# Second group norm of block 0: statistics as row sums instead of a statistics instruction

## The chip, the cores and the metric

The kernel runs on one core of a Trainium2 chip. A core has five engines that run side by side, each with its own in-order queue: TensorE (PE, matrix products), VectorE (DVE), ScalarE (ACT), GpSimd (POOL) and SyncE (SP), which here issues the DMAs. They wait for each other through semaphores. The metric is the time of one execution on the device, in microseconds; before the change the median of three runs is 7226.67 us.

## The reference

The input x is 4 images of 128 channels and 128 x 128 pixels, float32. Two layers follow each other.

Layer 0 turns an image into a sequence of 16384 tokens of 128 channels, sends it through a small MLP, an input projection, a causal convolution of 4 taps and a selective scan, and then

```
g  = out.reshape(B, 4, 32, H, W)
xn = (g - g.mean) * rsqrt(g.var + 1e-5)          # first group norm, 4 groups
x1 = silu(xn * gn_w + gn_b) + x
```

Layer 1 needs, beside a filter in the Fourier domain, one set of 4 weights for each image:

```
a = group_norm(concat([x1, x1]))                 # second group norm: 32 groups over 256 channels
a = relu(agg_w @ a + agg_b);  pooled = a.mean    # then a softmax over 4 logits
```

So the second group norm wants, for each channel of x1, its mean and its variance over 16384 pixels; channels are then combined to groups.

## The kernel before

The kernel has two blocks. Block 0 (line 150 on) computes layer 0 and, while a later image is scanned, also the first group norm, x1, the second group norm and the softmax weights of the image before. Block 1 computes the Fourier part; the last image's norms run there.

Block 0 works in chunks of 512 tokens, 32 for an image and 128 in all, numbered k. A chunk is cut into 16 slots. In each slot two tiles of 128 x 512 are scanned. The order of all instructions is written out by hand: lists `todo[slot, phase]` are filled first, and a double loop (L503 to L506) then issues slot after slot and, in a slot, phase after phase in the order of L504: turn, sums, pe, exps, late, act, pool, dbu, early, gate, scans, dve, end. Each engine sees its own instructions in that order. Slot numbers below count within a chunk.

What a slot does on each engine:
- ScalarE: the exponentials for the next slot's scans (`exps`, L392), small copies of scan states (L414 and L506), and whatever the phase act holds: activations of the next chunk, two for each (L238 u in slot 2, L252 xd in slot 4, L455 and L456 o in slot 5, L274 delta in slot 6, L303 bt in slots 8 to 14).
- VectorE: two scans (L411), and in odd slots mostly two products of a scanned tile with C (L413); the copies of L414 on ScalarE wait for them. In slots 2 and 10 a gating product (L442).
- GpSimd: products for the scans to come (`dbu`, L362) and products of scanned tiles with C that VectorE doesn't do (L418), and in slot 7 `du` (L311).
- TensorE: the projections, transposes and the sums over the state.

Which tiles' products VectorE takes is decided by `by_vector` (L346). In the chunks where the norm runs (`norming`, L337: k from 34 to 49, 66 to 81, 98 to 113) VectorE takes one product fewer than otherwise.

The norm of an image is `finish` (L560). It is called for images 0 to 2 in block 0 (L488 to L490) and for image 3 in block 1. It first calls `group_norm` (L509) for the first norm; its row sums and sums of squares come from `o_act` (L455 and L456), where ScalarE accumulates while it copies. Then, for each of 32 tiles i of 128 x 512, two tiles to a chunk: `norm_load` brings x and the layer's output from DRAM (slots 13 and 14 of the chunk before); `norm_act` (slot 2) applies scale, bias and Silu on ScalarE, into a PSUM bank; `norm_dve` (slot 3, phase dve) adds x on VectorE and stores x1 to DRAM; `norm_stats` (slot 3, phase end) runs one statistics instruction on the sum on VectorE (L593). Six numbers per tile are kept in `stats1`. Five slots after the last addition `group_norm` is called for the second norm: `aggregate` (L519) turns the 32 x 6 numbers into mean and variance on VectorE (L522), `mean_mm` multiplies by a matrix that averages over groups, and so on to the scale. For the first norm, `aggregate` adds up the 32 pairs of sums (L524), and `mean_mm` first forms mean and variance from them with four small operations on ScalarE (L529 to L532).

Of the kernel before, what the change touches and what calls it, by code (L numbers as in the profile page):

```python
# [26 lines left out]
F32 = mybir.dt.float32  # L27
AF = mybir.ActivationFunctionType
ALU = mybir.AluOpType
AX = mybir.AxisListType  # L30
# [3 lines left out]
P = 128  # L34
# [471 lines left out]
                        f()  # L506


def group_norm(s, io, b, mat, which, stat, at, then):  # L509


    nc = s.nc
    g = {}

    def small(n, m=1):
        g[n] = io.small.tile([P, m], F32, tag=n, name=f"{n}_{which}_{b}")
        return g[n]

    def aggregate():  # L519
        mv = small("mv", 2)  # L520
        if which:
            nc.vector.bn_aggr(mv, stat().rearrange("p n q -> p (n q)"))  # L522
        else:
            nc.vector.reduce_sum(mv, stat(), axis=AX.X)  # L524

    def mean_mm():
        if which == 0:
            mv, q = g["mv"], small("q")
            nc.scalar.activation(q, mv[:, 0:1], AF.Square, scale=1.0 / s.L)  # L529
            nc.scalar.mul(q, q, -1.0)  # L530
            nc.scalar.mul(mv[:, 0:1], mv[:, 0:1], 1.0 / s.L)
            nc.scalar.activation(mv[:, 1:2], mv[:, 1:2], AF.Identity, scale=1.0 / s.L, bias=q)  # L532
        ps = g["ps"] = io.psum(f"gm_{which}_{b}")
        nc.tensor.matmul(ps[:, 0:1], getattr(s, mat), g["mv"][:, 0:1], start=True, stop=True)

    def spread_act():
        mv = g["mv"]
        nc.scalar.copy(small("mean"), g["ps"][:, 0:1])
        q = small("q")
        nc.scalar.activation(q, mv[:, 0:1], AF.Square, scale=-1.0, bias=g["mean"])  # L540
        nc.scalar.activation(q, q, AF.Identity, bias=mv[:, 1:2])

    def var_mm():
        ps = g["ps"] = io.psum(f"gv_{which}_{b}")
        nc.tensor.matmul(ps[:, 0:1], getattr(s, mat), g["q"], start=True, stop=True)

    def root_act():
        nc.scalar.activation(small("rstd"), g["ps"][:, 0:1], AF.Sqrt, bias=s.eps)

    def invert():  # L550
        nc.vector.reciprocal(g["rstd"], g["rstd"])
        then(g["mean"], g["rstd"])

    return [
        (at, "dve", aggregate), (at, "end", mean_mm), (at + 1, "act", spread_act), (at + 3, "pe", var_mm),
        (at + 5, "act", root_act), (at + 6, "dve", invert),
    ]


def finish(s, io, b, first, norm, agg, add="dve"):  # L560

    nc, NCH, C, L, NF = s.nc, s.NCH, s.C, s.L, s.NF
    stats, outs = s.stats, s.outs
    g = {}

    def start(mean, rstd):
        for n in ("scale", "bias"):
            g[n] = io.small.tile([P, 1], F32, tag=n, name=f"{n}_{b}")  # L570
        nc.scalar.activation(g["scale"], s.gnw, AF.Identity, scale=rstd)
        nc.scalar.activation(g["bias"], mean, AF.Identity, scale=g["scale"])
        nc.scalar.activation(g["bias"], g["bias"], AF.Identity, scale=-1.0, bias=s.gnb)
        g["stat"] = io.small.tile([P, NCH, 6], F32, tag="stats1", name=f"stats1_{b}")

    def norm_load(i):
        xr = g["x", i] = io.big.tile([P, T], F32, tag="xr", name=f"xr_{b}_{i}")
        o = g["o", i] = io.big.tile([P, T], F32, tag="o", name=f"of_{b}_{i}", bufs=io.bufs)
        nc.sync.dma_start(out=xr, in_=s.xflat[b, :, i * T : (i + 1) * T])
        nc.sync.dma_start(out=o, in_=outs[b][:, i * T : (i + 1) * T])  # L580

    def norm_act(i):

        g["n", i] = io.psum(f"n_{b}_{i}")
        nc.scalar.activation(g["n", i], g["o", i], AF.Silu, bias=g["bias"], scale=g["scale"])

    def norm_dve(i):
        o = g["o", i]
        nc.vector.tensor_add(o, g.pop(("n", i)), g.pop(("x", i)))
        nc.sync.dma_start(out=s.x1flat[b][:, i * T : (i + 1) * T], in_=o)  # L590

    def norm_stats(i):
        nc.vector.bn_stats(g["stat"][:, i, :], g.pop(("o", i)))  # L593

    def middle(mean, rstd):
        g["mean"] = mean
        g["weff"] = io.small.tile([P, C], F32, tag="weff", name=f"weff_{b}")
        nc.scalar.activation(g["weff"], s.weff0, AF.Identity, scale=rstd)
        g["acc"] = io.small.tile([P, NCH], F32, tag="acc", name=f"acc_{b}")

    def bias_mm():
        g["ps"] = io.psum(f"bv_{b}")
        nc.tensor.matmul(g["ps"][:, 0:1], g["weff"], g["mean"], start=True, stop=True)

    def bias_act():
        g["bv"] = io.small.tile([P, 1], F32, tag="bv", name=f"bv_{b}")
        nc.scalar.activation(g["bv"], g["ps"][:, 0:1], AF.Identity, scale=-1.0, bias=s.bias0)

    def agg_load(i):
        x1 = g["x1", i] = io.big.tile([P, T], F32, tag="xr", name=f"x1_{b}_{i}")  # L610
        nc.sync.dma_start(out=x1, in_=s.x1flat[b][:, i * T : (i + 1) * T])

    def agg_mm(i, home):
        ps = g["pa", i] = (home or io.psum)(f"agg_{b}_{i}")
        nc.tensor.matmul(ps, g["weff"], g.pop(("x1", i)), start=True, stop=True)  # L615

    def agg_act(i):
        ps = g.pop(("pa", i))
        nc.scalar.activation(ps, ps, AF.Relu, bias=g["bv"], accum_out=g["acc"][:, i : i + 1])

    def pool_dve():
        g["pooled"] = io.small.tile([P, 1], F32, tag="pooled", name=f"pooled_{b}")
        nc.vector.reduce_sum(g["pooled"], g["acc"], axis=AX.X)

    def pool_act():
        g["pbc"] = io.small.tile([P, P], F32, tag="pbc", name=f"pbc_{b}")
        nc.scalar.activation(g["pbc"], s.ones, AF.Identity, scale=g["pooled"])

    def logits_mm():
        g["ps"] = io.psum(f"lg_{b}")  # L630
        nc.tensor.matmul(g["ps"][:, 0:NF], g["pbc"], s.wwg, start=True, stop=True)

    def logits_dve():
        lg = g["lg"] = io.small.tile([P, NF], F32, tag="lg", name=f"lg_{b}")
        mx = g["mx"] = io.small.tile([P, 1], F32, tag="mx", name=f"mx_{b}")
        nc.vector.scalar_tensor_tensor(lg, g["ps"][:, 0:NF], 1.0 / L, s.bwg, ALU.mult, ALU.add)
        nc.vector.reduce_max(mx, lg, axis=AX.X)

    def softmax_act():
        mx, lg = g["mx"], g["lg"]  # L640
        nc.scalar.mul(mx, mx, -1.0)
        total = g["total"] = io.small.tile([P, 1], F32, tag="total", name=f"total_{b}")
        nc.scalar.activation(lg, lg, AF.Exp, bias=mx, accum_out=total)

    def softmax_dve():
        nc.vector.reciprocal(g["total"], g["total"])

    def weights_act():
        nc.scalar.activation(s.wts[b], g["lg"], AF.Identity, scale=g["total"])

    todo = group_norm(s, io, b, "g0", 0, lambda: stats[b], first, start)
    for i in range(NCH):
        at = norm(i)
        todo += [
            (at[0], "pe", partial(norm_load, i)), (at[1], "act", partial(norm_act, i)),
            (at[2], add, partial(norm_dve, i)), (at[2], "end", partial(norm_stats, i)),
        ]
    c = at[2] + 5
    todo += group_norm(s, io, b, "g1", 1, lambda: g["stat"], c, middle)
    todo += [(c + 7, "pe", bias_mm), (c + 8, "act", bias_act)]  # L660
    for i in range(NCH):
        at = agg(i)
        todo += [
            (at[0], "dve", partial(agg_load, i)), (at[1], "pe", partial(agg_mm, i, at[3])),
            (at[2], "act", partial(agg_act, i)),
        ]
    c = at[2] + 1
    return todo + [
        (c, "dve", pool_dve), (c + 1, "act", pool_act), (c + 4, "pe", logits_mm), (c + 4, "dve", logits_dve),
        (c + 5, "act", softmax_act), (c + 6, "dve", softmax_dve), (c + 7, "act", weights_act),  # L670
    ]


def block1(tc, s):
# [7 lines left out]
    nc, B, C, H, W, WF, NF, NCH = s.nc, s.B, s.C, s.H, s.W, s.WF, s.NF, s.NCH  # L682
    HH = H // 2
    filt = s.a["filt_w"].rearrange("f c h w q -> h f c (w q)")
    with ExitStack() as ctx:
        def pool(name, bufs, **kw):
# [15 lines left out]
        io = SimpleNamespace(  # L702
            big=pool("big", 4), bufs=4, small=small, psum=lambda n: psf.tile([P, T], F32, tag="pf", name=f"pf_{n}")
        )
# [4 lines left out]

        t1 = norm(NCH - 1)[2] + 14  # L710
        todo = defaultdict(list)
        steps = finish(s, io, B - 1, 0, norm, lambda i: (t1 + i - 3, t1 + i, t1 + i, None), "add")
        for at, phase, f in steps:
            todo[at, phase].append(f)
        spare = max(at for at, _ in todo) // 3 + 2
# [23 lines left out]
        for k, ft in enumerate(spans):  # L739
            at = max(ft.first - 4, min(k, 1))  # L740
# [243 lines left out]
```

## Time and profile before

| | |
|---|---|
| median of three runs | 7226.67 us (7223.53 to 7229.71) |
| the profiled execution: span from its first to its last instruction | 7219.4 us |
| VectorE busy | 6925.4 us (96%), 8040 instructions |
| GpSimd busy | 6890.8 us (95%), 3188 instructions |
| ScalarE busy | 6133.6 us (85%), 13583 instructions |
| TensorE busy | 5935.8 us (82%) |
| the addition L589: in block 0, in block 1 | 96 at 678 ns, 32 at 681 ns |
| the statistics L593: both blocks | 128 at 681 ns |
| a scan, L411 (the largest group) | 1976 at 1265 ns |

The profiled execution has no time of its own beside its span; what a run has around the span is to be seen only as the difference to the median, 7.3 us. Busy time leaves out the waiting of an engine, so an engine at 96% over the whole may have no idle time at all in one stage; durations of neighbours overlap by a little, so what an instruction costs is better read from one start to the next than from its length.

### The profile page before, as it was taken

Reading aid. Unit: us, or ns where it says so; the run is one execution under the profiler, and the core shown is the slowest. Engines: PE = TensorE matmul, PEld = TensorE weight load, DVE = VectorE, ACT = ScalarE, POOL = GpSimd, SP = SyncE. Lnnn points to the kernel's source line nnn. Section 1 sums busy time; section 2 is a strip of 40 time slices with the busy share of each in tenths; the row PEclk is TensorE's granted clock in tenths of the full one; section 3 lists DMA queues with packets and bytes.
Section 4 is the critical chain, followed back from the end, with each engine's and each line's share of the span. In section 5 each row is a group of like instructions: output and inputs, shape, how many; then the busy total and the mean of one; then the engine's idle time right before and its main releaser. Section 6 shows DMA issues by size and latency. Waiting matters only on the chain. (4 is left out here: it accounts for less than half of the span.)

```text
span 7219.4 us, 89408 instructions
## 1 busy us (share of the span) xinstructions
PE 5935.8 (82%) x25908; PEld 2629.2 (36%) x25908; DVE 6925.4 (96%) x8040; ACT 6133.6 (85%) x13583; POOL 6890.8 (95%) x3188
## 2 busy tenths in 40 slices
PE   7888888888878788888788788887787888868999
PEld 2333333322222233332222233332232323348999
DVE  7999999999999999999999999999999999978677
ACT  7888888888888888888888888888888888877876
POOL 7999999999999999999999999999999999977787
PEclk8888888888888898998888899998888898989999
DMA  6766676677777776777777777777787777768666
GB/s 151 160 159 160 151 165 159 151 165 172 180 192 178 182 172 161 175 169 170 190 179 192 174 160 176 171 160 187 179 192 181 169 173 169 161 167 240 183 169 164
DMA packets 864127, 1246.27 MB, mean 173 GB/s; under 512 B 78856, under 2 KB 318608, under 8 KB 863632
## 3 DMA queue, kind: packets, MB, share of 16 engines
q1 hardware_dynamic: 863488, 1240.28, 71.8%
q8 instruction: 204, 3.34, 0.2%
q14 instruction: 291, 2.38, 0.1%
q10 hardware_dynamic: 144, 0.26, 0.0%
HBM read 996.97 MB, written 243.27 MB: 172 GB/s over the span
## 5 line engine op out<-in xcount | busy, mean ns | idle before, releaser
L362 POOL TENSOR_TENSOR hb<-rdu,rB 128x1536 f32<-128x1536 f32 (+2 forms) x1536 | 3608.0, 2366 | 35.1 <-DMA rdu<-dd 32.1
L392 ACT ACTIVATE da<-rdelta,amat 128x512 f32<-128x512 f32 x4096 | 2786.1, 698 | 139.3 <-DVE h L411 134.5
L418 POOL TENSOR_TENSOR hb<-h,rC 128x1024 f32<-128x1024 f32 (+1 forms) x1072 | 2436.8, 2275 | 68.4 <-DVE h L411 53.9
L411 DVE TENSOR_TENSOR_SCAN da<-da,st,hb 128x512 f32<-128x512 f32 x1976 | 2417.4, 1265 | 22.1 <-ACT da L392 15.6
L432 PE MATMUL y<-hb,sel 128*32 128x512 f32 x8192 | 1337.9, 730 | 4.7 <-POOL hb L418 4.1
L382 PE MATMUL b<-ident,bt 128*128 128x128 f32 x4096 | 753.9, 307 | 673.5 <-DVE h L411 539.1
L413 DVE TENSOR_TENSOR hb<-da,rC 128x512 f32<-128x512 f32 x2040 | 1294.3, 672 | 3.0
L411 DVE TENSOR_TENSOR_SCAN h<-da,st,b 128x512 f32<-128x512 f32 x992 | 1256.2, 1266 | 1.5 <-PE b L382 1.5
L411 DVE TENSOR_TENSOR_SCAN h<-da,st,hb 128x512 f32<-128x512 f32 x1000 | 1249.9, 1254 | 1.4 <-ACT da L392 1.0
L233 PE MATMUL pp_cv<-xm,wck 128*128 128x512 f32 x2048 | 1061.0, 665 | 1.4 <-ACT xm L216 0.8
L303 ACT ACTIVATE bt<-pt_dut,xdt 128x256 f32<-128x256 f32 x2048 | 836.3, 470 | 186.0 <-PE pt_dut L292 185.8
L382 PEld LDWEIGHTS b<-ident,bt 128*128 128x128 f32 x4096 | 525.5, 154 | 1242.1 <-DVE h L411 902.5
L414 ACT COPY st<-da 128x1 f32<-128x1 f32 x2040 | 271.3, 159 | 495.0 <-DVE hb L413 494.7
L233 PEld LDWEIGHTS pp_cv<-xm,wck 128*128 128x128 f32 x2048 | 417.3, 215 | 706.5 <-issue 460.8
L767 POOL TENSOR_TENSOR wb<-wb,term 128x1040 f32<-128x1040 f32 x192 | 461.1, 2402 | 89.8 <-ACT term L761 78.6
L292 PE MATMUL pt_dut<-ident,du 128*128 128x128 f32 x1024 | 233.7, 339 | 299.9 <-ACT xdt L285 174.0
L428 PE MATMUL y<-u,diag 128*128 128x512 f32 x512 | 300.9, 671 | 149.7 <-DVE zs L442 147.6
L292 PEld LDWEIGHTS pt_dut<-ident,du 128*128 128x128 f32 x1024 | 132.5, 163 | 618.6 <-POOL du L311 492.3
L392 ACT ACT_TABLE_LOAD x262 | 336.1, 1283 | 11.8 <-DMA rdelta<-dd 7.1
L311 POOL TENSOR_TENSOR du<-delta,u 128x512 f32<-128x512 f32 x256 | 319.6, 1271 | 26.7 <-ACT delta L274 26.7
L432 PEld LDWEIGHTS y<-hb,sel 128*32 128x32 f32 x8192 | 173.3, 116 | 371.4 <-issue 278.0
L266 PE MATMUL pp_dt<-xd,wdt 8*128 8x512 f32 x512 | 281.9, 639 | 31.9 <-ACT pp_o L456 23.4
(145 smaller groups left out, 8082.0 us busy)
## 6 DMA issues: line engine op xcount, KB each, us to landing
rdelta<-dd SPq DMA_DIRECT2D x1024, 256.0 KB, 4.7
rdu<-dd SPq DMA_DIRECT2D x1024, 256.0 KB, 7.8
rC<-bc SPq DMA_DIRECT2D x512, 256.0 KB, 7.5
rB<-bc SPq DMA_DIRECT2D x512, 192.0 KB, 4.7
dd<-delta SPq DMA_DIRECT2D x256, 256.0 KB, 7.4
dd<-du SPq DMA_DIRECT2D x256, 256.0 KB, 5.9
ft<-in_filt_w SPq DMA_DIRECT2D x104, 520.0 KB, 6.9
ob<-o SPq DMA_DIRECT2D x128, 256.0 KB, 2.0
```

The costliest lines, as they stand in the source:

```text
L233: nc.tensor.matmul(ps["cv", j], w, d["xm"][:, t : t + T], start=t == 0, stop=t == KC - 1)
L292: nc.tensor.transpose(ps["dut"][:, 2 * t + j, :], d["du"][:, j, at : at + P], s.ident)
L303: nc.scalar.activation(d["bt"][:, 2 * h + t, :, q, :], src, AF.Copy, scale=d["xdt"][:, 2 * h + t, R + q : R + q + 1])
L311: nc.gpsimd.tensor_tensor(du, d["delta"][:, j, :], d["u"][:, j, :], ALU.mult)
L362: nc.gpsimd.tensor_tensor(hb[:, p : p + n, :], d["du", j][:, m : m + n, :], d["B"][:, p - 1 : p - 1 + n, :], ALU.mult)
L382: nc.tensor.transpose(b[:, t * P : (t + 1) * P], src, s.ident)
L392: nc.scalar.activation(da, d["delta", j][:, m, :], AF.Exp, scale=s.amat[:, c : c + 1])
L411: nc.vector.tensor_tensor_scan(o, das[q], b, init, ALU.mult, ALU.add)
L413: nc.vector.tensor_tensor(hb[:, p + q, :], das[q], d["C"][:, p + q, :], ALU.mult)
L418: nc.gpsimd.tensor_tensor(hb[:, ps, :], h[:, q, :], d["C"][:, ps, :], ALU.mult)
L432: nc.tensor.matmul(y[m * DG : (m + 1) * DG, :], s.sel, d["hb", j, r][:, p, :], start=False, stop=r == NG - 1)
L767: nc.gpsimd.tensor_tensor(wb, wb, u[n].terms[f], ALU.add)
```

## The change

`finish` and `group_norm` get an argument `sums`. It is true for images 0 to 2 in block 0, and false for the last image in block 1, which keeps the statistics instruction. With `sums`:
- `norm_dve` no longer adds with `tensor_add` but with `tensor_tensor_reduce`, which writes the same sum tile and, in a column of `stats1`, the sum of each row.
- `norm_stats` is no longer the statistics instruction on VectorE but a Square on ScalarE that accumulates each row's sum of squares into `stats1`. It stands one slot later (slot 4) and in the phase act, behind the copy of xd. Its elementwise output goes into the tile of x, which is therefore kept until then.
- `stats1` is 128 x 2 x 32 instead of 128 x 32 x 6, and the second norm's `aggregate` and `mean_mm` work as those of the first norm do: one row sum on VectorE, and four small operations on ScalarE.

`by_vector` and `norming` stay as they are.

```diff
-def group_norm(s, io, b, mat, which, stat, at, then):
+def group_norm(s, io, b, mat, which, stat, at, then, sums):
     def aggregate():
         mv = small("mv", 2)
-        if which:
+        if sums:
+            nc.vector.reduce_sum(mv, stat(), axis=AX.X)
+        else:
             nc.vector.bn_aggr(mv, stat().rearrange("p n q -> p (n q)"))
-        else:
-            nc.vector.reduce_sum(mv, stat(), axis=AX.X)
     def mean_mm():
-        if which == 0:
+        if sums:
             mv, q = g["mv"], small("q")
...
-def finish(s, io, b, first, norm, agg, add="dve"):
+def finish(s, io, b, first, norm, agg, add="dve", sums=True):
...
-        g["stat"] = io.small.tile([P, NCH, 6], F32, tag="stats1", name=f"stats1_{b}")
+        shape = [P, 2, NCH] if sums else [P, NCH, 6]
+        g["stat"] = io.small.tile(shape, F32, tag="stats1", name=f"stats1_{b}")
...
     def norm_dve(i):
-        o = g["o", i]
-        nc.vector.tensor_add(o, g.pop(("n", i)), g.pop(("x", i)))
+        o, n = g["o", i], g.pop(("n", i))
+        if sums:
+            total = g["stat"][:, 0, i : i + 1]
+            nc.vector.tensor_tensor_reduce(o, n, g["x", i], 1.0, 0.0, ALU.add, ALU.add, total)
+        else:
+            nc.vector.tensor_add(o, n, g.pop(("x", i)))
         nc.sync.dma_start(out=s.x1flat[b][:, i * T : (i + 1) * T], in_=o)

     def norm_stats(i):
-        nc.vector.bn_stats(g["stat"][:, i, :], g.pop(("o", i)))
+        o = g.pop(("o", i))
+        if sums:
+            nc.scalar.activation(g.pop(("x", i)), o, AF.Square, accum_out=g["stat"][:, 1, i : i + 1])
+        else:
+            nc.vector.bn_stats(g["stat"][:, i, :], o)
...
-            (at[2], add, partial(norm_dve, i)), (at[2], "end", partial(norm_stats, i)),
+            (at[2], add, partial(norm_dve, i)), (at[2] + sums, "act" if sums else "end", partial(norm_stats, i)),
...
-        steps = finish(s, io, B - 1, 0, norm, lambda i: (t1 + i - 3, t1 + i, t1 + i, None), "add")
+        steps = finish(s, io, B - 1, 0, norm, lambda i: (t1 + i - 3, t1 + i, t1 + i, None), "add", False)
```

More of the change, by code (lines that the diff above doesn't have):

```diff
@@ L649, in weights_act @@
         nc.scalar.activation(s.wts[b], g["lg"], AF.Identity, scale=g["total"])
-    todo = group_norm(s, io, b, "g0", 0, lambda: stats[b], first, start)
+    todo = group_norm(s, io, b, "g0", 0, lambda: stats[b], first, start, True)
     for i in range(NCH):
@@ L655, in finish @@
             (at[0], "pe", partial(norm_load, i)), (at[1], "act", partial(norm_act, i)),
-            (at[2], add, partial(norm_dve, i)), (at[2], "end", partial(norm_stats, i)),
+            (at[2], add, partial(norm_dve, i)), (at[2] + sums, "act" if sums else "end", partial(norm_stats, i)),
         ]
     c = at[2] + 5
-    todo += group_norm(s, io, b, "g1", 1, lambda: g["stat"], c, middle)
+    todo += group_norm(s, io, b, "g1", 1, lambda: g["stat"], c, middle, sums)
     todo += [(c + 7, "pe", bias_mm), (c + 8, "act", bias_act)]
```

## The prediction, made before the change was run

> **What bounds the kernel now.** I read the page's first part first: the span, and how long each engine was busy.
>
> ```profile
> span 7219.4 us, 89408 instructions
> PE 5935.8 (82%) x25908; PEld 2629.2 (36%) x25908; DVE 6925.4 (96%) x8040; ACT 6133.6 (85%) x13583; POOL 6890.8 (95%) x3188
> ```
>
> VectorE (DVE) and GpSimd (POOL) are both nearly full, so the question is which has slack where the change works. The change touches chunks 34 to 49, 66 to 81 and 98 to 113 of block 0, 48 in all, two additions and two statistics in each. I took the sums over two stretches, cut at the ends of VectorE's second gating product (L442): two chunks without the norm, and chunk 40 with it.
>
> ```profile
> core 0: us, PE busy (x) PEld busy (x) DVE busy (x) ACT busy (x) POOL busy (x), PEclk, DMA share, GB/s
> 523.00:620.48 97.48, 79.82 (x308) 29.28 (x304) 97.45 (x102) 83.69 (x188) 96.62 (x45) 0.87 0.69 158
> 2025.52:2075.81 50.29, 38.81 (x153) 13.92 (x152) 50.26 (x55) 43.23 (x96) 50.08 (x24) 0.93 0.77 185
> ```
>
> In chunk 40 VectorE is idle for 0.03 us, GpSimd for 0.21 us, ScalarE (ACT) for 7.06 us. VectorE sets the pace, with GpSimd 0.21 us behind. So what VectorE saves cannot all come out, and ScalarE's 7 us must be looked at by place. The timeline of the two engines in that chunk (start, length, engine, line, count, idle time before and who ended it), VectorE first:
>
> ```profile
> 2028.99 1.28 DVE L589 TENSOR_TENSOR of<-pp_n,xr 128x512 f32<-128x512 f32 x2
> 2030.19 1.27 DVE L593 BATCH_NORM_STATS2 stats<-of 128x6 f32<-128x512 f32 x2
> 2031.39 1.26 DVE L411 TENSOR_TENSOR_SCAN h<-da,st,b 128x512 f32<-128x512 f32 x1
> ...
> 2044.36 1.25 DVE L411 TENSOR_TENSOR_SCAN h<-da,st,hb 128x512 f32<-128x512 f32 x1
> 2045.53 2.43 DVE L411 TENSOR_TENSOR_SCAN da<-da,st,hb 128x512 f32<-128x512 f32 x2
> ```
>
> ```profile
> 2022.62 0.16 ACT L414 COPY st<-da 128x1 f32<-128x1 f32 x1 [0.44 <-DVE hb L413]
> ...
> 2032.93 0.58 ACT L252 COPY xd<-pt_xd 40x512 f32<-40x512 f32 x1
> 2033.85 0.69 ACT L392 ACTIVATE da<-rdelta,amat 128x512 f32<-128x512 f32 x1 [0.34 <-DVE h L411]
> ...
> 2036.79 0.16 ACT L414 COPY st<-da 128x1 f32<-128x1 f32 x1 [0.33 <-DVE hb L413]
> 2037.38 0.16 ACT L414 COPY st<-da 128x1 f32<-128x1 f32 x1 [0.44 <-DVE hb L413]
> ...
> 2044.33 1.30 ACT L392 ACTIVATE da<-rdelta,amat 128x512 f32<-128x512 f32 x2
> ```
>
> The reader is to see a loop. ScalarE leaves its wait for VectorE's last product of slot 1 at 2022.62. From there to the exponentials of slot 9 (2044.33, the first done at about 2045.02) it is without a break but for 0.34 + 0.33 + 0.44 = 1.11 us, all spent waiting for VectorE. Slot 9's first scan takes that exponential at 2045.53, 0.51 us later. Everywhere else ScalarE's lead is larger or ends in a wait for VectorE. The same chain holds 1.07 to 1.12 us of waits in each of chunks 34 to 49. GpSimd waits in this chunk once for VectorE (and 0.05 us in one gap without a named cause):
>
> ```profile
> 2039.79 2.35 POOL L418 TENSOR_TENSOR hb<-h,rC 128x1024 f32<-128x1024 f32 x1 [0.16 <-DVE h L411]
> ```
>
> For prices, groups of ScalarE over the whole span, by shape (count | busy us, mean ns):
>
> ```profile
> L241 ACT ACTIVATE zs<-zs 128x1024 f32<-128x1024 f32 x128 | 135.3, 1057 | 1.4
> L456 ACT ACTIVATE pp_o<-pp_o 128x512 f32<-128x512 f32 x128 | 74.6, 583 | 0.0
> L456 ACT ACTIVATION_READ_ACCUMULATOR pp_o<-pp_o 128x1 f32 x128 | 23.9, 187 | 0.0
> ```
>
> [...] On GpSimd: [...] here 1024 more elements take 2168 ns (1280 ns for 512, 3448 for 1536), 2.12 ns each, so a lighter VectorE will not make GpSimd quicker.
>
> **The change, part by part.** Start to start, VectorE's two statistics take 2031.39 − 2030.19 = 1.20 us. They go: −1.20 us of VectorE in each of 48 chunks, 58 us.
>
> The two additions (1.20 us start to start) each become an addition that sums its row. The trace has no such instruction, so I bound its extra cost d: from below 0, since no two-input 128x512 instruction here is quicker than the plain one; from above the rate of the scan, (2.43 − 1.25) − 0.60 = 0.58 us, with ScalarE's 0.19 us for a read of the accumulator on top, 0.77 us. I take 0.1 us: full rate, and a 128x1 instruction, the shortest kind here (the reciprocal of L551 has 147 ns, of which some 0.07 to 0.12 us aren't overlapped). VectorE's own work in a chunk becomes 50.26 − 1.20 + 0.20 = 49.26 us.
>
> ScalarE gets two squares with accumulation, SBUF to SBUF, at the end of slot 4's phase, behind the copy of xd at 2032.93. It needs no new table: L456's squares sit between exponentials without a load. One costs s: [...] the read adds what it adds in L455/L456, where a 598 ns copy of the same size takes 0.48 us start to start and an accumulating one 0.58 to 0.61 us, so 0.11 us. s = 0.64 us. Ends: 0.53 (the read free) and 0.80 us (priced as the 779 ns Silu of L585, 0.70 us start to start, plus the read). The squares wait for additions done at about 2030.3 plus 2d, and ScalarE gets there at 2033.5: no wait. Queued behind them are the exponential of slot 6, the copy-out of o (L455, L456), and the exponentials of slot 7, the softplus of delta and the exponentials of slots 8 and 9.
>
> Now the loop. ScalarE from 2022.62 to 2045.02 is 22.40 us, 21.29 without waits. VectorE reaches slot 4 a whole 1.00 us earlier, so those three waits are over. With the squares it is 21.29 + 1.28 = 22.57 us, 0.17 us more than now; but 0.51 us of lead was there to lose, of which 0.05 us goes to the semaphore. Slot 9 can start 0.51 − 0.05 − 0.17 = 0.29 us earlier than now. VectorE itself would be ready 1.00 us earlier, so it waits for ScalarE some 0.7 us, in slots 8 and 9. The other stretch of the loop, VectorE from slot 9 to slot 1 of the next chunk, is unchanged. The chunk goes from 50.29 to 50.00 us; 48 × 0.29 = 13.9 us.
>
> GpSimd's floor is 50.08 us a chunk, so over 16 chunks it falls 16 × 0.08 = 1.3 us behind. In chunk 34 it is idle for 3.10 us, 2.95 of them waiting for the slot-4 scan that stands behind the removed statistics, so it regains 1.0 us there, and its smallest lead before a scan that needs its product (slot 14's replacement for the next chunk) is 1.4 us. It just fits.
>
> TensorE: its second dt product waits for the copy-out of o, which ends 0.94 us later in the chunk; the softplus comes at its place 2.3 us behind that product's end, and TensorE has 11 us idle in the chunk: nothing. DMAs: no new ones and none moved in SP's queue; the xr and o buffers come free a slot (3 us) later and are loaded again nine slots on: nothing, and with fewer slots between, the load would move onto SP's queue.
>
> The aggregation falls from 0.92 to 0.12 us start to start (L522, L524), and four small operations join ScalarE (0.69 us in chunk 65, L529 to L532), three times. There VectorE waits anyway (1.02 us in chunk 81): I take zero, within 2 us either way.
>
> Sum: 7219.4 − 13.9 = 7205.5 us for the profiled execution. The median of the runs shown, 7226.67 us, is 7.3 us above the span (launch and end); I keep those: 7212.8, 7213 us.
>
> **The rivals.** 0.2% of the time (14.5 us) is about what a measurement of this kernel can tell from no change.
> - ScalarE's loop binds, as above: 7208 to 7219 us by s from 0.60 to 0.70. Chance 0.56, half of it beyond 0.2%.
> - GpSimd binds without using its lead: 48 × 0.21 = 10 us, 7217 us. Its 0.21 us of idle time speaks for it, its lead of 1.4 us against. 0.10.
> - Nothing comes out: s near 0.785, where 2s eats the 0.29 us too, or an addition at the scan's rate (d = 0.58, 1.16 of 1.20 us given back): 7222 to 7231 us. 0.10.
> - Slower: the summing addition runs at the scan's rate and its read is not overlapped, d = 0.77. VectorE alone then needs 50.26 − 1.20 + 1.54 = 50.60 us, 0.34 more: 48 × 0.34 = 16 us, 7243 us. It decides from d = 0.60 on, and passes 0.2% at 0.75[...]. For it: the trace has no price. [...] 0.16.
> - More than forecast: squares cheap and GpSimd catching up to its limit, (16 × 0.21 + 1.0 + 1.4) × 3 = 17 us, with the aggregation 19 to 20: 7207 us; VectorE's whole 48 us (7179 us) only if GpSimd became quicker. 0.08.
>
> **How the numbers follow.** Faster 0.28 + 0.08 = 0.36; same 0.28 + 0.10 + 0.10 = 0.48; slower 0.16. From 7204 to 7232 us lie the first three cases and half the last: 0.80. The forecast's own range is 7208 to 7219.
>
> **What would show it.** Right: chunk 40 at 50.0 us; VectorE idle about 0.7 us in it, ended by ScalarE's exponentials in slots 8 and 9; GpSimd idle near 0; squares at 630 ns and no table load on their line; the three waits of ScalarE gone. Wrong: an addition over 1.1 us; VectorE's waits named GpSimd instead; ScalarE waiting in front of the squares; or a difference that lies outside these 48 chunks.

## The result, and the profile after

The changed kernel takes 7208.57 us, median of 10 runs (7199.20 to 7216.11), against 7226.20 us for the kernel before, median of 10 runs beside them (7222.97 to 7229.71): 17.6 us less, a ratio of 0.9974 with the interval 0.9965 to 0.9983. Forecast were 7213 us and a range of 7204 to 7232. A second series gave 7203.62 us and 0.9975 (0.9966 to 0.9984). The head of the page of the changed kernel, span and busy time by engine:

```profile
span 7207.0 us, 89666 instructions
PE 5987.7 (83%) x25908; PEld 2655.0 (37%) x25908; DVE 6888.4 (96%) x8040; ACT 6181.7 (86%) x13787; POOL 6890.0 (96%) x3188
```

VectorE has lost 37 us of busy time, ScalarE has gained 48, GpSimd is where it was (6890.8 us then, 6890.0 now). The instructions of the new addition, line 592 (count: duration in ns, min/median/max):

```profile
L592 DVE CUSTOM_DVE_ANT_0 of<-pp_n,xr x96: 675/681/689, 1735.1 to 5662.9; 128x512 f32<-128x512 f32 x96
L592 DVE DVE_READ_ACCUMULATOR2_ANT stats<- x96: 76/81/87, 1735.7 to 5663.5; 128x1 f32 x96
```

It has the 681 ns that the plain addition had in block 1, and an 81 ns read behind it. In chunk 38 VectorE's timeline shows that the read costs almost nothing (start, length, engine, line, count, idle time before and its end):

```profile
1934.24 0.68 DVE L592 CUSTOM_DVE_ANT_0 of<-pp_n,xr 128x512 f32<-128x512 f32 x1
1934.85 0.08 DVE L592 DVE_READ_ACCUMULATOR2_ANT stats<- 128x1 f32 x1
...
1950.18 2.47 DVE L411 TENSOR_TENSOR_SCAN da<-da,st,hb 128x512 f32<-128x512 f32 x2 [0.35 <-ACT da L392]
```

The second addition starts at 1934.85 too, and the scan behind it at 1935.46: 0.61 us from one to the next, where the plain one took 0.60. The last line is the first scan of slot 9, the only place in this chunk where VectorE waits, and it waits for ScalarE's exponential. ScalarE's timeline of the same chunk shows why:

```profile
1927.87 0.16 ACT L414 COPY st<-da 128x1 f32<-128x1 f32 x1 [0.44 <-DVE hb L413]
...
1938.19 0.57 ACT L252 COPY xd<-pt_xd 40x512 f32<-40x512 f32 x1
1938.66 0.62 ACT L600 ACTIVATE xr<-of 128x512 f32<-128x512 f32 x1
1939.19 0.19 ACT L600 ACTIVATION_READ_ACCUMULATOR xr<-of 128x1 f32 x1
...
1939.89 0.67 ACT L392 ACTIVATE da<-rdelta,amat 128x512 f32<-128x512 f32 x1
...
1949.45 1.30 ACT L392 ACTIVATE da<-rdelta,amat 128x512 f32<-128x512 f32 x2
```

Two squares take 1939.89 − 1938.66 = 1.23 us, with no table load among the records of L600 (96 squares of 620 ns, 96 reads of 189). From 1927.87 to the first exponential of slot 9, done at 1950.14, ScalarE waits for nothing: the three waits of 0.34, 0.33 and 0.44 us are gone, as forecast.

An early and a late chunk of the norm of the first image (36 and 45; columns as in the windows of before):

```profile
core 0: us, PE busy (x) PEld busy (x) DVE busy (x) ACT busy (x) POOL busy (x), PEclk, DMA share, GB/s
1831.33:1881.05 49.72, 39.53 (x152) 14.22 (x152) 49.32 (x54) 44.19 (x100) 49.72 (x24) 0.90 0.78 187
2279.76:2329.76 50.00, 39.58 (x157) 15.16 (x155) 49.42 (x54) 44.06 (x100) 50.00 (x24) 0.90 0.76 186
```

Before, each of these took 50.29 us. Now there are two regimes. Chunks 35 to 40 take 49.72 us; chunk 41 takes 49.80, and from chunk 42 on it is 49.97 to 50.03. (Chunk 34, the first, takes 50.02, with two small waits more.) GpSimd is busy without a gap in both rows. In the late regime a second wait joins; chunk 42 on VectorE:

```profile
2149.14 2.47 DVE L411 TENSOR_TENSOR_SCAN da<-da,st,hb 128x512 f32<-128x512 f32 x2 [0.34 <-ACT da L392]
...
2172.01 1.28 DVE L411 TENSOR_TENSOR_SCAN h<-da,st,hb 128x512 f32<-128x512 f32 x1 [0.21 <-POOL hb L362]
```

The scan of slot 14 now waits for GpSimd's product: the lead that GpSimd had over the scans that need its products is spent. The other two images behave alike (49.72 us for six or seven chunks, then 50.0). Over the 45 chunks 34 to 48, 66 to 80 and 98 to 112 that is 18.56 us less than before.

The two profiled executions differ by 12.4 us of span, not 18.6. Summed by place: these 45 chunks −18.56; chunks 49, 81 and 113, where the second norm is aggregated, +2.51; the stretch up to the end of chunk 0 +8.48; all the rest −4.8. In chunk 81 VectorE waits longer for ScalarE than before (0.99 us then, one wait), and 1.02 us for TensorE, for which it didn't wait then. The waits for ScalarE:

```profile
4103.69 1.28 DVE L411 TENSOR_TENSOR_SCAN h<-da,st,hb 128x512 f32<-128x512 f32 x1 [0.74 <-ACT da L392]
...
4111.35 2.46 DVE L411 TENSOR_TENSOR_SCAN da<-da,st,hb 128x512 f32<-128x512 f32 x2 [2.04 <-ACT da L392]
```

The 8.48 us lie far from the change, 1.6 ms ahead of its first instruction. Most of them are one pair of VectorE instructions in chunk 0, which form a weight for block 1. Before:

```profile
78.50 1.14 DVE L134 TENSOR_SCALAR weff<-wagg,gn_gamma 128x128 f32<-128x128 f32 x1
79.68 3.42 DVE L135 SCALAR_TENSOR_TENSOR weff<-wagg,gn_gamma,weff 128x128 f32<-128x128 f32 x1
```

After:

```profile
79.75 10.38 DVE L134 TENSOR_SCALAR weff<-wagg,gn_gamma 128x128 f32<-128x128 f32 x1
90.16 0.35 DVE L135 SCALAR_TENSOR_TENSOR weff<-wagg,gn_gamma,weff 128x128 f32<-128x128 f32 x1
```

Together 4.56 us then and 10.73 now, 6.2 us more for the same work. GpSimd's timeline beside these instructions, before and then after, which the last experiment needs:

```profile
77.07 2.49 POOL L311 TENSOR_TENSOR du<-delta,u 128x512 f32<-128x512 f32 x2
79.51 3.44 POOL L362 TENSOR_TENSOR hb<-rdu,rB 128x1536 f32<-128x1536 f32 x1
```

```profile
86.48 3.57 POOL L362 TENSOR_TENSOR hb<-rdu,rB 128x512 f32<-128x512 f32 x2
```

The rest of the 8.48 is a slower start of TensorE (1.2 us), a gap of VectorE of 0.96 us that no wait in the profile explains, and small change.

### The profile page after: what moved, and what is told of

Its sections match the earlier page's. It is cut to its first block, busy times and chain, and to the rows that moved or that the text cites. A ratio compares the mean times of both kernels' runs of the same rounds, so it can differ in the third digit from the quotient of the medians.

```text
span 7207.0 us, 89666 instructions
## 1 busy us (share of the span) xinstructions
PE 5987.7 (83%) x25908; PEld 2655.0 (37%) x25908; DVE 6888.4 (96%) x8040; ACT 6181.7 (86%) x13787; POOL 6890.0 (96%) x3188
## 5 line engine op out<-in xcount | busy, mean ns | idle before, releaser
L362 POOL TENSOR_TENSOR hb<-rdu,rB 128x1536 f32<-128x1536 f32 (+2 forms) x1536 | 3610.9, 2368 | 27.4 <-DMA rdu<-dd 26.0
L432 PE MATMUL y<-hb,sel 128*32 128x512 f32 x8192 | 1372.7, 737 | 14.6 <-POOL hb L418 12.4
L266 PE MATMUL pp_dt<-xd,wdt 8*128 8x512 f32 x512 | 304.7, 687 | 114.7 <-ACT pp_o L456 92.2
```

Of the source, the lines that this page charges most:

```text
L362: nc.gpsimd.tensor_tensor(hb[:, p : p + n, :], d["du", j][:, m : m + n, :], d["B"][:, p - 1 : p - 1 + n, :], ALU.mult)
L432: nc.tensor.matmul(y[m * DG : (m + 1) * DG, :], s.sel, d["hb", j, r][:, p, :], start=False, stop=r == NG - 1)
```

## The experiments

The theory: in the norm's chunks the time is first set by the loop ScalarE → VectorE → ScalarE (27.38 us of VectorE from slot 9 to slot 1, 22.28 us of ScalarE from there to slot 9's exponential, 0.03 us for each handover: 49.72), and once GpSimd's lead is spent, by GpSimd's 50.00 us. Its rivals: the squares' own cost holds the chunk, or the sum of VectorE's work.

### Without the squares

Left out are the 96 squares; the second norm's variance comes from a constant and is not computed.

```diff
+        if sums:
+            nc.vector.memset(g["stat"][:, 1, :], 1024.0)
...
-            nc.scalar.activation(g.pop(("x", i)), o, AF.Square, accum_out=g["stat"][:, 1, i : i + 1])
+            g.pop(("x", i))
```

> The kernel after, with the 96 squares of block 0 left out (so the variance of the second norm isn't computed; a constant stands in its place). Theory: two limits one after the other. In chunks 35 to 40 the kernel after runs at 49.72 us, the length of the loop through ScalarE; from chunk 42 on at 50.0 us, GpSimd's own work, since by then VectorE has used up its lead of about 2 us over GpSimd. Without the squares VectorE alone needs about 49.2 us, the lead is used in two or three chunks, and the rest runs at 50.0 us: no more than 3 us from the kernel after (7205 to 7212 us). Rival: ScalarE's loop is the only limit, and GpSimd's lack of idle time a coincidence: 49.2 us in all 48 chunks, 0.66 us less than after on average, 7175 to 7180 us.

Measured: 7203.58 us (7198.41 to 7209.46), ratio 0.9969 (0.9957 to 0.9980). Chunks 34 and 45:

```profile
1724.07:1773.21 49.14, 40.75 (x152) 15.01 (x151) 49.10 (x54) 43.07 (x96) 47.21 (x22) 0.83 0.79 189
2272.09:2322.10 50.01, 40.71 (x150) 14.90 (x151) 49.24 (x55) 42.97 (x96) 50.01 (x24) 0.83 0.75 185
```

The first row is VectorE's own work, 49.14 us with nothing else in the way. It lasts two chunks; the third takes 49.57, and from the fourth on it is GpSimd's 50.0. The 45 chunks save 18.88 us, against 18.56 with the squares. So the loop through ScalarE decides how quickly GpSimd's lead is spent, and GpSimd decides how much is saved in all. The chunks came as forecast; the median didn't quite. It is 5.0 us below the changed kernel's 7208.57, where at most 3 had been forecast, and level with that kernel's second series.

### The squares added to the kernel before

Additions and statistics stay; the squares are computed as well, in slot 4, into a column that nothing reads.

```diff
+    def norm_squares(i):
+        nc.scalar.activation(x, o, AF.Square, accum_out=g["sq"][:, i : i + 1])
...
+            (at[2] + 1, "act", partial(norm_squares, i)),
```

> The kernel before, with ScalarE's 96 squares added in slot 4 beside the statistics, which stay on VectorE. Theory: the squares take 1.23 us of ScalarE in a chunk, its three waits for VectorE (1.11 us, and some 0.24 us of lost overlap behind them) give that back, and what is left is within the 0.51 us of lead before slot 9: chunks stay at 50.29 us, and the time within 3 us of before. Rival: any work in that stretch of ScalarE delays slot 9, so 1.23 us a chunk are lost: 59 us, 7285 us.

Measured: 7227.64 us (7224.76 to 7230.17), ratio 1.0001 (0.9993 to 1.0010). The chunks take 50.30 us throughout, and the 45 of them 0.36 us more than before. ScalarE's timeline there:

```profile
2038.36 0.57 ACT L252 COPY xd<-pt_xd 40x512 f32<-40x512 f32 x1
2038.84 0.62 ACT L599 ACTIVATE xr<-of 128x512 f32<-128x512 f32 x1
...
2040.07 0.67 ACT L392 ACTIVATE da<-rdelta,amat 128x512 f32<-128x512 f32 x1
```

The two squares take 2040.07 − 2038.84 = 1.23 us, and the wait in front of the exponential (0.34 us before) is gone. ScalarE's waits and its 0.51 us of lead do hide two squares at 1.23 us. That is the term of the sum by itself: added work at no cost where VectorE binds.

### The squares moved out of the loop

In the changed kernel the squares go to slot 11, behind the loop's exponentials; those of the last two tiles stay in slot 4.

```diff
-(at[2] + sums, "act" if sums else "end", partial(norm_stats, i)),
+(at[2] + (sums and (8 if i < NCH - 2 else 1)), "act" if sums else "end", partial(norm_stats, i)),
```

> The kernel after, with the squares issued in slot 11 instead of slot 4 (those of the last two tiles stay in slot 4), where ScalarE has 1.3 us of idle time in a wait for TensorE. Theory: the wait of VectorE in slot 9 goes, but the chunk is then set by GpSimd at 50.0 us once the lead is used; within 4 us of the kernel after. Rival (ScalarE's loop alone): 49.2 us in all chunks, 7175 to 7180 us.

Measured: 7198.25 us (7195.05 to 7211.10), ratio 0.9965 (0.9952 to 0.9978). Chunks 34 and 45:

```profile
1721.51:1770.65 49.14, 41.05 (x159) 15.59 (x157) 49.11 (x55) 44.28 (x100) 47.21 (x22) 0.90 0.78 189
2269.57:2319.62 50.05, 40.29 (x151) 14.95 (x150) 49.37 (x55) 43.98 (x100) 50.05 (x24) 0.86 0.75 185
```

With all the squares there, it is the picture without them: 49.14, 49.14, 49.57, then 50.0, and 18.58 us saved. Where the squares stand decides whether ScalarE's loop binds; that they exist does not. And it brings the 45 chunks nothing, since GpSimd takes over sooner. The median is 10.3 us below the changed kernel's first and 5.4 below its second, more than the 4 us forecast. The chunks don't hold that difference: of the profiled spans' 10.6 us, 10.4 lie before the end of chunk 0, where the stall of the changed kernel is missing here.

### A product given back to VectorE

If GpSimd's load is the limit, taking a product from it should raise the gain; if the loop is, putting that product on VectorE's stretch of it should cost. In all norm chunks VectorE gets back the product that it doesn't do there:

```diff
             if norming(k):
-                return p > 1 and (j, r, p) != (1, 2, 2)
+                return p > 1
```

> The kernel after, with the one product that VectorE leaves to GpSimd in chunks with the norm (half 1, group 2, position 2, in slot 13) given back to VectorE. GpSimd's work falls by 1.08 us to about 48.9 us a chunk, VectorE's stretch from slot 9 to slot 1 grows by 0.60 us. Theory: that stretch is part of the loop through ScalarE, so the loop takes 49.72 + 0.60 = 50.3 us in all chunks: as slow as before the change (7222 to 7230 us), GpSimd idle for over 1 us a chunk. Rival: GpSimd alone is the limit after the change and VectorE's wait for ScalarE would yield: VectorE's own 49.2 + 0.6 = 49.8 us, faster than after by some 5 us.

Measured: 7222.11 us (7216.44 to 7228.05), ratio 0.9996 (0.9987 to 1.0004). Chunk 36:

```profile
1880.88:1931.07 50.19, 39.93 (x153) 14.50 (x151) 49.82 (x56) 44.27 (x100) 49.25 (x23) 0.86 0.77 185
```

GpSimd has 0.9 us to spare (over 1 us had been forecast) and VectorE 0.37 us, and still most chunks take 50.17 to 50.19 us (some 50.3 to 50.7, the last one of two images 51.3 to 51.4): neither engine's load holds them. The 45 chunks come out 0.5 us below the kernel before. VectorE's idle time is one wait of 0.34 us in slot 9 for the exponential, as in the changed kernel. The loop is 27.83 + 0.03 + 22.28 + 0.03 = 50.17, if the product adds 0.45 us to VectorE's stretch; I had forecast 50.3, with a product's whole 0.6 us. The timelines show the difference: that slot takes VectorE 5.45 us in the changed kernel (1960.23 to 1965.68) and 5.90 with the second product (1910.35 to 1916.25). Alone, the product directly follows the scan that it reads and starts 0.03 us after its end (1965.04, 1965.07); with two, the other one's scan and product lie between, and nothing stands.

### Both: out of the loop, and balanced

Neither of the two edits alone shortens the 45 chunks of the changed kernel: moving the squares meets GpSimd, relieving GpSimd meets the loop. Together they should leave VectorE as the bound. The squares stand in slot 11, and VectorE takes the product back in every second chunk:

```diff
-                return p > 1 and (j, r, p) != (1, 2, 2)
+                return p > 1 and ((j, r, p) != (1, 2, 2) or k % 2 == 0)
```

It ran beside a repetition of the changed kernel.

> The kernel after, unchanged, for its time beside the three that follow on the same chip, and for a second profile. Expected: chunks 35 to 40 at 49.72 us and 42 to 48 at 50.0 us again; the tensor_scalar of the 128x128 product in slot 8 of chunk 0 (line 134) has taken 10.4 us in three profiles and 1.1 us in three others, so either may come.

> The kernel after with the squares in slot 11, and with the product of slot 13 given back to VectorE in every second chunk with the norm. Theory: with the squares out of the loop only VectorE's own work (49.14 us, plus 0.60 us in every second chunk: 49.44 us on average) and GpSimd's (50.0 us less 0.54 us on average: 49.46 us, of which the lead takes off another 0.12 us) are left, and they are even: 49.45 us a chunk, 0.42 us less than after, 45 chunks: 19 us faster than the kernel after. Rival: the ScalarE loop has another limit near 49.7 us that the squares hid; then no gain over the run with the squares in slot 11 alone (some 5 to 10 us below after).

Measured: the changed kernel again 7203.62 us (7198.56 to 7213.17), ratio 0.9975 (0.9966 to 0.9984), its chunks again 49.72 and then 50.0, its 45 chunks −18.82 us. Two early chunks of its second image took 50.2 to 50.3, and there 49.72 lasted four chunks longer; the image's sum was the same to 0.1 us, which fits a lead that was used up later. The balanced one 7180.87 us (7175.43 to 7182.40), ratio 0.9940 (0.9927 to 0.9952). Chunks 45 and 46 of it:

```profile
2264.12:2313.26 49.14, 39.71 (x152) 14.54 (x152) 49.11 (x55) 44.33 (x100) 49.14 (x23) 0.86 0.78 189
2313.26:2362.86 49.60, 39.31 (x152) 14.65 (x152) 49.60 (x56) 44.21 (x100) 49.60 (x24) 0.90 0.77 188
```

The chunks alternate between 49.14 and 49.59 us, to the end of the norm; over both, VectorE is busy for 98.71 of 98.74 us and waits for nobody; GpSimd has no gap either, so the two are even. Their mean is 49.37 (forecast 49.45), the 45 chunks save 40.69 us, 21.9 more than those of the changed kernel, and the kernel is 22.7 us faster than that one beside it (forecast 19). This version beats both kernels, and it confirms the two limits in turn: removing both releases what neither edit released alone.

### The stall in chunk 0

My theory was that VectorE waits for GpSimd inside the two instructions of L134 and L135, and that their form, a scalar read from SBUF for each row, is why. So the scaling went to ScalarE, and one plain addition stayed on VectorE; once in the changed kernel, once in the balanced one.

```diff
-        nc.vector.tensor_scalar_mul(weff0, s.wagg[:, 0, :], s.gam[:, 0:1])
-        nc.vector.scalar_tensor_tensor(weff0, s.wagg[:, 1, :], s.gam[:, 1:2], weff0, ALU.mult, ALU.add)
+        nc.scalar.activation(weff0, s.wagg[:, 0, :], AF.Copy, scale=s.gam[:, 0:1])
+        nc.scalar.activation(part, s.wagg[:, 1, :], AF.Copy, scale=s.gam[:, 1:2])
+        nc.vector.tensor_tensor(weff0, weff0, part, ALU.add)
```

> The kernel after with the 128x128 product of slot 8 in chunk 0 (lines 134 and 135) computed as two ScalarE copies with a scale and one VectorE addition. Theory: the tensor_scalar and the scalar_tensor_tensor wait inside their own duration for GpSimd, 4.6 us together in one way and 10.7 us in another; an addition of two SBUF tensors doesn't (VectorE's 2040 products beside GpSimd are all near 672 ns). Expected: the addition under 0.5 us, the time 4 to 10 us below the kernel after, its spread from run to run smaller by about 6 us. Rival: what VectorE loses there is regained later (GpSimd catches up) or the spread comes from elsewhere: no gain, the spread as before.

> Both edits of the two runs before together. Theory: the gains add up, 23 to 29 us below the kernel after. Rival: one takes the place of the other, no more than 20 us.

Measured: 7208.47 us (7202.76 to 7220.83), ratio 0.9979 (0.9972 to 0.9987); the balanced one 7182.79 us (7180.74 to 7185.90), ratio 0.9945 (0.9932 to 0.9957). Neither gains. The addition in the first of them:

```profile
81.56 7.30 DVE L137 TENSOR_TENSOR weff<-weff,part 128x128 f32<-128x128 f32 x1 [3.06 <-ACT part L136]
```

One half of the theory fell: the stall doesn't need that form. A plain addition of two 128x128 tiles lasts 7.30 us there (7.28 in the other). In the profiled executions the long stall (10.4 us) is there in the changed kernel, in its repetition, with the squares added and with the product given back; it isn't (1.1 and 3.4 us, as before) without the squares, with the squares moved and in the balanced kernel.

The other half, that VectorE waits for GpSimd inside the instruction, fits the four profiles in which GpSimd's timeline lies beside these instructions: both kernels, the squares moved, and the first of these two runs. In the kernel before, L134 ends at 79.64, 0.08 us behind GpSimd's `du`, and L135 at 83.10, 0.15 us behind the L362 that ran beside it. In the changed kernel L134 ends at 90.13, 0.08 us behind GpSimd's last L362; GpSimd then stands for 6.29 us, since it waits for VectorE's scan, and L135, done in that time, takes 0.35 us. In all four each of these instructions that lasts over 1 us ends 0.08 to 0.15 us behind the end of a GpSimd instruction, and those of 7.30 and 10.38 us end only when GpSimd has nothing left to do: it stands for 5.97 and for 6.29 us then. The 672 ns products that the expectation leaned on are no counterexample: each reads one input from PSUM (`da`, from the pool `psd` in `exps`), while the addition put in here reads both from SBUF. Whether that is what matters was not tested; no run moved these instructions to a place where GpSimd is idle, and why GpSimd goes on ahead of VectorE in one program and not in another stays open.

The stall makes 6.2 us of difference between kernels that have the same instructions at that place, and so a comparison of medians between these versions is uncertain by that much; the readings above rest on chunk lengths for this reason.

## Why the prediction was right, point by point

- **The bound.** Right: VectorE set the pace of these chunks, and behind it stood two more limits, ScalarE's loop and GpSimd's 50 us, both below what VectorE saved. That a lighter VectorE would not make GpSimd quicker was my estimate; GpSimd was busy for 6890.8 us before and for 6890.0 us after. VectorE's own chunk is 49.14 us (forecast 49.26, with d at 0.1).
- **The summing addition.** I took d = 0.1 us between ends of below 0 and 0.77; it is 0.01 (0.61 us from one start to the next, against 0.60). That the sum leaves the addition at its rate was my estimate, and nothing in the trace of before showed it; the addition, with one input in PSUM and one in SBUF, keeps 681 ns, where a scan of the same 128x512 takes 1265. The second instruction was an estimate after ScalarE's pair of them; the trace shows it on VectorE too, a read of 81 ns, and that it is hidden. The rival "slower" was excluded by this number alone.
- **The squares.** Forecast 0.64 us each, no table load, no wait in front; measured 0.615 us, no table load, no wait. The 630 ns for the square itself are 620. These 630 ns and the 0.53 us from its start to the next were my estimate, and no square of 128x512 from SBUF to SBUF stood in the trace of before to show them; the 0.53 us came out (1938.66 to 1939.19).
- **The loop.** The mechanism was right and its size was not: 50.00 forecast, 49.72 measured. ScalarE's stretch is 22.28 us where I had 22.57. The squares account for 0.05 of it. The other 0.24 us went missing in the step "21.29 without waits": I subtracted the three waits alone. In chunk 38 of the changed kernel the ScalarE instructions that follow their predecessor without a wait start 0.03 to 0.11 us before its recorded end (the first square at 1938.66, the copy ahead of it ends at 1938.19 + 0.57 = 1938.76), but for those next to a table load, 0.01 to 0.02 us behind; one that waited doesn't (before, the exponential at 2033.85 starts 0.34 us behind the end of the copy of xd, 2032.93 + 0.58 = 2033.51). Three waits less are 0.24 us more, 0.08 us each on average.
- **VectorE's waits.** I expected 0.7 us in slots 8 and 9; there are 0.35 us, in slot 9, for the exponential.
- **GpSimd's lead.** "It just fits" was the wrong step, in consequence: a loop of 49.72 instead of 50.00 lies below GpSimd's floor and eats the lead. The floor is 50.00 us (forecast 50.08), and the lead that was used up is 15 × 0.29 = 4.35 us less than the 6.2 us that an image's 15 chunks save, so 1.8 to 1.9 us. I had put the smallest lead at 1.4 us in the early chunks. Thus two of my cases hold one after the other, ScalarE's loop for six or seven chunks and GpSimd at its limit for the rest, and the sum is 18.6 us in place of 13.9. The 17 us that I had worked out for the second of them, with a chance of 0.08, was the better number.
- **The aggregation.** Forecast zero within 2 us; the three chunks cost 2.51 us, and 3.95 in the repetition: outside. It isn't the four small operations alone: without the squares, which leaves those four in, the three chunks cost 0.01 us. Which combination it is was not tested; over the other versions with these four operations the three chunks lie between 3.7 us less and 2.9 us more than before.
- **Nothing elsewhere.** Not so: the 6.2 us stall in chunk 0, which no step had; it ends 0.08 us behind the last GpSimd instruction ahead of a stand of 6.29 us, and what starts it is open. Between the two profiled executions it took back a third of the gain.
- **Span and median.** The 7.3 us around the span were wrong. A profiled execution of the changed kernel took 7208.82 us with a span of 7207.0, so 1.8 us. By that measure the profile of before came from an execution some 5 us quicker than its median. It did no harm, since the forecast was in effect the median less the gain.

With sizes in place: 7226.2 − 18.6 (the chunks) + 2.5 (the aggregation) + 6.2 (the stall) is 7216 us, and the median is 7208.57. The remaining 7 to 8 us lie in stretches without the norm; they are within what single executions differ by (the runs of the changed kernel spread over 17 us, those of the kernel before beside them over 7). So it is partly luck that the median came within 4.4 us of the forecast: the chunks gave 4.7 us more than forecast, the aggregation and the stall took 8.7 back in the profiled execution, and 7 to 8 us that I neither forecast nor can explain made up for it. The four quickest of the ten, 7199 to 7202 us, have a granted clock of 0.885 to 0.887 over the whole execution, the other six, 7208 to 7216 us, one of 0.877 to 0.881; whether that is the cause was not tested.

## What to carry to other kernels

When work is taken off the engine that sets the pace, list every limit just behind it, with each one's floor and lead: here the limit of 50.00 us, with its lead, showed only from chunk 42 on, the ninth of the first image, so read the last repetitions as well as the first. Two limits of nearly the same size, 49.72 and 50.00 us, hid each other here: the 45 chunks saved 18.56 us in the changed kernel, 18.58 and 0.5 us with an edit against either, and 40.69 us with the pair; only the pair showed what both were worth. When a wait disappears from a chain, give back, beside the wait, the overlap of the instruction that had waited (here 0.08 us for each of three).

## What was unexpected of the hardware

- A VectorE addition of 128x512 that also sums its rows costs 0.61 us from start to start, against 0.60 for the plain one, both with one input in PSUM; the 81 ns read of the sum lies beside the next instruction.
- On ScalarE the three waits that went returned about 0.08 us each, on average, beside their own length.
- A small VectorE instruction in chunk 0 lasts 1.1 us in one program and 10.4 us in another that is the same at that place, and a plain addition put there lasted 7.3 us; each ends within 0.15 us of the end of a GpSimd instruction, and L135 takes 3.4 us beside a busy GpSimd and 0.35 beside one that stands.
